# Layer 1 of a four-layer kernel: norm products queued behind an image, x1 stores on two queues, other places in SBUF, a band's weights side by side

## The chip, the cores and the metric

The kernel runs on one core of a Trainium2 chip. A core has five engines, each of which executes its own instructions in order: PE (the matrix engine), DVE and ACT (vector and scalar arithmetic), POOL (general) and SP (which here only issues DMA transfers; POOL and ACT can issue them too). Times are device microseconds (us) of one launch. Lower is better.

## The reference

An input x of shape (4, 8, 512, 512), read as T=4 time steps, B=8 channels and 512 x 512 pixels, goes through four residual layers. Each normalises x by groups of channels (four groups of two), applies an operator and adds the result to x:

```python
x = x + L0(_gn(x))   # spiking attention: q, k, v, scores + relative bias, projection
x = x + L1(_gn(x))   # 13x13 Gaussian, each of the 8 channels by itself, reflected edges
x = x + L2(_gn(x))   # quantised 3x3 convolution, 8 to 8 channels
x = x + L3(_gn(x))   # 3x3 convolution, 8 to 8 channels
```

```python
def _gn(v, G=4, eps=1e-5):
    B_, C_, H_, W_ = v.shape
    g = v.reshape(B_, G, C_ // G, H_, W_)
    m = jnp.mean(g, axis=(2, 3, 4), keepdims=True)
    s = jnp.var(g, axis=(2, 3, 4), keepdims=True)
    return ((g - m) / jnp.sqrt(s + eps)).reshape(v.shape)
```

## The kernel before

Layer 0 runs over 32 steps (b, t), each one attention on one image. Tables of the relative bias (table_own, L476, issued by SP; table_x) are streamed in during each step. What a step leaves is x1, the input of layer 1, written by `project_out` in four chunks c of 128 rows: PE adds up ps_out, ACT copies the input (L862), DVE adds the spikes (L874) and mirrors the edge columns (L879), and DMAs store the rows (L882) and the mirrored edge rows (L887, L890) in DRAM. A step stores 36 pieces and 12 edge rows. In the last two steps, (7,2) and (7,3), which the code calls `late`, POOL issues all of them. The first three chunks of (7,3) lie in a tile of their own, x1_last.

Layer 1 is the class `Layer1`: 32 images n = 4b + t in order. An image lies in one of three buffers xs[n % 3]; `load_image` fills it by four DMAs, and for the first three images a fifth (L1248) fills the spare rows. xs[0] is a part of a tile called raw, which also holds eye (the identity, added to the bands) and the first image's weights bt.

The convolution is made of products with bands: for each image, DVE first forms bt = band · r + eye (L1258; r is 1/deviation of the image's group), then differences d of neighbouring columns in four pieces, two for each half image j (tiles d of a pool d1 of four). PE forms in each half the groups x,bt (odd), d,bt (odd) and d,bt (even), each of 8 matmuls (L1356); the even part of a half is issued after the first group of the next half, from a list `due`. Image 0 is done "plainly" (L1369), without d. ACT moves the results to xo; DVE takes the largest and the smallest value of each half; eight DMAs (L1436) store xo as x2, issued by SP for b = 0 and by POOL for all later b.

```python
if plain:
    self.fetch(1)
    self.offset(0)
self.fetch(n + 2)
```

So image n + 2 is asked for with image n, and `prepare(n + 1)` makes the next bt and d between the halves of image n.

`next_norm(g - 1)` computes the norm of x2's group g - 1 in steps: DVE's sums (L1476 to L1482, L194, L196), a product gps_x on PE (L199) that adds over partitions, DVE again, a second gps_x, and a power on POOL. `group` advances it by t steps after image t of the first channel of group g.

The order of the work is set in three ways. Instructions go to their engine's queue in the order that a list scheduler finds from the program and its priorities. `in_turn` chains those of layer 1 on each engine, by `tc.issue_after(op)`, which places an instruction behind op on op's engine; `self.tails` holds the last of each engine. The framework adds the waits between engines, from the tiles that instructions read and write; a tile that lies over an older tile's place in SBUF waits for the older one's readers and stores.

Where the places overlap before: image 1's buffer x1_0 is at bytes 65696 to 82464 of each partition, d1 (four pieces) at 82464 to 115744, image 2's buffer x1_1 at 115744 to 132512, bt1 at 132512 to 138016. In layer 0, the bias tables lie at 65696 to 97952, x1_last at 112288 to 118576, and the input rows of the last step at 124576 to 132768.

The bands come from `bands1`, run in step n = 1 of layer 0: one DMA (L1214) copies the band rows from SBUF to 16 slanted places in the DRAM array band1d, over a fill with zeros. `start_layer1` loads band1d (L1009) at the end of layer 0. In band1d a row holds, for each of 16 output rows, first the channel, then the pixel offset, then the six bands; the six bands of one pixel are neighbours, so that one band's 64 weights of a matmul lie six elements apart.

Of the kernel before, what the change touches and what calls it, by code (L numbers as in the profile page):

```python
# [35 lines left out]
F32 = mybir.dt.float32  # L36
# [5 lines left out]
ALU = mybir.AluOpType  # L42
# [3 lines left out]
P = 128  # L46
# [11 lines left out]
K1, R1 = 13, 6  # L58
# [234 lines left out]
def layer0(  # L293
# [532 lines left out]
    def project_out(so, c, xt, b, t):  # L826


        dst = x1d[t][b]
        ps = ps_mm.tile([P, D], F32, tag="mm", name="ps_out")  # L830
        late = b == B - 1 and t >= T - 2
        pool_, tag, n_bufs = (x_raw, "sums", 3) if late else (work, "so", 1)
        tokens = pool_.tile([P, NC, P], F32R, tag=tag, name="so", bufs=n_bufs)
        with tc.issue_after(placed[-1]) if placed and not late else ExitStack():
            nc.scalar.copy(tokens, so[:, :, t % 2, ::-1][:, :, c * P : (c + 1) * P])
        nc.scalar.copy(ps, c_p)  # L836
        for k in range(NC):
            for z in range(2):
                nc.tensor.matmul(  # L839
                    ps, lhsT=tokens[:, k, :], rhs=wpT[z][:, k, :],  # L840
                    start=False, stop=k == NC - 1 and z == 1, skip_group_check=True,
                )
        h = h_of["p"][:, c, :]
        if x1_last and c < 3:
            x1 = x1_last[0][:, c]
        else:
            x1 = x1p.tile([P, PH, X1_U], F32, tag="x1", name=f"x1s_{b}_{t}_{c}")
        flat = x1.rearrange("p f u -> p (f u)")
        odd = bass.AP(
            flat.tensor, flat.offset + X1_E + 1,  # L850
            [flat.ap[0], [2 * X1_U - 1, 2], [X1_U, 2], [1, NV // 2]],
        )
        halves = [
            (
                xt.rearrange("p (k g) -> p g k", g=2 * PH)[:, 2 : 2 + PH],
                x1[:, :, 1 : 1 + NV // 2],
            ),
            (xt.rearrange("p (k q f) -> p q f k", q=PH, f=2)[:, ::-3], odd),
        ]
        for x, own in halves:  # L860
            with tc.issue_after(seeds[-1]):
                op = nc.scalar.copy(own, x)  # L862
        placed.append(op.ins)
        v = work.tile([P, D], F32, tag="v", name="v_p", bufs=2)
        if t == 0:
            nc.vector.tensor_copy(v, ps)
        else:
            nc.vector.scalar_tensor_tensor(v, h, 0.5, ps, op0=ALU.mult, op1=ALU.add)
        for z, (_, own) in enumerate(halves):
            cut = v[:, z * HN : (z + 1) * HN]  # L870
            cut = cut.rearrange("p (f k) -> p f k", f=PH)
            parts = [(cut, own)] if z == 0 else [(cut[:, 2 * e : 2 * e + 2], own[:, e]) for e in range(2)]
            for on, to in parts:
                nc.vector.scalar_tensor_tensor(to, on, 1.0, to, op0=ALU.is_ge, op1=ALU.add)  # L874
            nc.vector.bn_stats(st1[b // PAIR][:, t, b % PAIR, c, z, :], own)
        if t < T - 1:
            nc.vector.scalar_tensor_tensor(h, v, 1.0, v, op0=ALU.is_lt, op1=ALU.mult)
        for to, of in MIRRORED:
            (nc.vector if late else nc.gpsimd).tensor_copy(pair(flat, *to), pair(flat, *of))  # L879
        cuts = [0, *range(W1_OUT - R1, P, W1_OUT), P]  # L880
        for first, end in zip(cuts, cuts[1:]):
            op = nc.gpsimd.dma_start(x1_rows(dst, R1 + c * P + first, end - first), x1[first:end])  # L882
        stored.append(op.ins)
        edge = nc.gpsimd if late else nc.sync
        for n in range(R1):
            if c == 0:
                edge.dma_start(x1_rows(dst, n, 1), x1[R1 - n : R1 - n + 1])  # L887
            if c == NC - 1:
                row = P - 1 - R1 + n
                edge.dma_start(x1_rows(dst, X1_R - 1 - n, 1), x1[row : row + 1])  # L890
# [101 lines left out]

    def start_layer1():

        band = shared.tile([P, W1_OUT, B, PH, BANDS], F32, tag="sums", name="band1")
        n_x, n_b = W1_N * X1_U, W1_OUT * BANDS * PH
        raw = shared.tile([P, n_x + 2 * n_b], F32, tag="raw", name="x1_0_0")
        x = raw[:, :n_x].rearrange("p (w u) -> p w u", u=X1_U)
        eye, bt = (
            raw[:, n_x + k * n_b : n_x + (k + 1) * n_b].rearrange("p (m z) -> p m z", z=BANDS)  # L1000
            for k in range(2)
        )
        load_image(nc, x, x1d[0][0], True)
        nc.sync.dma_start(
            eye.rearrange("p m z -> p (m z)"), i["c128"][:, i["c128"].shape[1] - n_b :]
        )
        own = band.rearrange("p r c o z -> p (r c o z)")
        for k in range(2):
            nc.sync.dma_start(by_row(own, k, M1, own.ap[1:]), band1d[k * M1 : (k + 1) * M1])  # L1009
        scale = small0.tile([P, 2], F32, name="scale_1")  # L1010
        nc.vector.tensor_copy(scale[:, 0:1], r1[:, 0, 0:1])
        nc.vector.tensor_scalar_mul(scale[:, 1:2], scale[:, 0:1], -1.0)
        for z in range(SHIFTS):
            out, same = (x[:, :, z].rearrange("p (r o) -> p r o", o=PH) for x in (bt, eye))
            nc.vector.scalar_tensor_tensor(
                out, band[:, :, 0, :, z], scale[:, z % 2 : z % 2 + 1], same,
                op0=ALU.mult, op1=ALU.subtract if z % 2 else ALU.add,
            )
        return band, eye, x, bt
# [153 lines left out]
def bands1(tc, i, band1d, w_sum, psum, state):  # L1173
# [37 lines left out]
    for z in (0, 2):  # L1211
        nc.vector.tensor_sub(to[:, :, SHIFTS + z // 2], to[:, :, z], to[:, :, z + 1])
    row = W1_OUT * n_m
    nc.sync.dma_start(  # L1214
        bass.AP(band1d.tensor, band1d.offset, [[row, n_p], [PH * row + n_m, W1_OUT], [1, n_m]]),
        band.unsqueeze(1).to_broadcast([n_p, W1_OUT, n_m]),
    )

    nc.vector.tensor_reduce(rows, w1, AX.X, ALU.add)
    nc.vector.memset(zeros[:K1, :], 1.0)  # L1220
# [8 lines left out]
    return bass.AP(own.tensor, own.offset + first * step, [[2 * step, n], *dims])  # L1229


def load_image(nc, xt, src, fill=False):

    size, n_half, n = X1_W * X1_U, W1_N // 2, N_PS1 * X1_U
    flat = xt.rearrange("p w u -> p (w u)")
    for j in range(N_1):
        for k, n_rows in ((0, M1), (1, K1_P - M1)):
            at = flat[:, j * n :]
            nc.sync.dma_start(
                by_row(at, k, n_rows, [[n_half * X1_U, 2], [1, n]]),  # L1240
                bass.AP(
                    src.tensor, src.offset + (k + j * N_PS1) * X1_U,
                    [[size, n_rows], [n_half * X1_U, 2], [1, n]],
                ),
            )
    if fill:
        n_rows, n = P - K1_P, W1_N * X1_U
        nc.sync.dma_start(  # L1248
            by_row(flat, 2 * (K1_P - M1) + 1, n_rows, [[1, n]]),
            bass.AP(src.tensor, src.offset, [[size, n_rows], [1, n]]),  # L1250
        )


def image_bands(nc, bt, band, b, r, eye):

    out, same = (x.rearrange("p (r o) z -> p r (o z)", o=PH) for x in (bt, eye))
    own = band[:, :, b].rearrange("p r o z -> p r (o z)")
    return nc.vector.scalar_tensor_tensor(out, own, r, same, op0=ALU.mult, op1=ALU.add)  # L1258


class Layer1:
    def __init__(
# [6 lines left out]
        )  # L1269
        self.band, self.eye, x, self.bt, self.stored = head  # L1270
        self.ps_c = s.enter_context(pool("ps_c", 6, space=PSUM))
        self.xs = [x]
        for k in range(2):
            if k == 1:
                self.dp = s.enter_context(pool("d1", 4))
            held = s.enter_context(pool(f"x1_{k}"))
            self.xs.append(held.tile([P, W1_N, X1_U], F32, name=f"x1_{k}"))
        self.bp = s.enter_context(pool("bt1", 2))
        self.op = s.enter_context(pool("o1", 2))
        self.ends, self.sums, self.offs, self.ready = {}, {}, {}, {}  # L1280
        self.last_ends, self.due, self.tails = [], [], {}
# [7 lines left out]
    def fetch(self, n):  # L1289
        if n < B * T:  # L1290
            b, t = divmod(n, T)
            load_image(self.nc, self.xs[n % 3], self.x1d[t][b], n < 3)

    def prepare(self, n):

# [6 lines left out]
        if t == 0:  # L1302
            self.offset(b)
        xt = self.xs[n % 3]
        bt = self.bp.tile([P, M1, BANDS], F32, tag="bt", name=f"bt_{b}_{t}", bufs=3)
        parts = [
            self.dp.tile([P, 2, N_PS1, 2, X1_E - 1], F32, tag="d", name=f"d_{b}_{t}_{j}")
            for j in range(N_1)
        ]
        self.ready[n] = bt, parts  # L1310
# [24 lines left out]
    def image(self, g, b, t):  # L1335
# [16 lines left out]
        def products(ps, bands, src, start):  # L1352

            for z in range(2):
                for q in range(2):
                    mm = nc.tensor.matmul(  # L1356
                        ps[q * M1 : (q + 1) * M1, :], lhsT=bt[:, :, bands[z]],
                        rhs=src(q)[:, :, z : z + n_v],
                        start=start and z == 0, stop=z == 1, skip_group_check=True,
                    )  # L1360
# [2 lines left out]
        def plainly(ps, par, j):  # L1363

            for z in range(SHIFTS):
                at = (par + z) % 2 * X1_E + (par + z) // 2
                for q in range(2):
                    w0 = q * n_half + j * N_PS1
                    mm = nc.tensor.matmul(  # L1369
                        ps[q * M1 : (q + 1) * M1, :], lhsT=bt[:, :, z],  # L1370
                        rhs=xt[:, w0 : w0 + N_PS1, at : at + n_v],
                        start=z == 0, stop=z == SHIFTS - 1, skip_group_check=True,
                    )
# [70 lines left out]
    def group(self, g):  # L1444
# [9 lines left out]
        for b in range(g * PAIR, (g + 1) * PAIR):  # L1454
            for t in range(T):
# [3 lines left out]
                if g > 0 and b % PAIR == 0 and t > 0:  # L1459
                    if t == 1:  # L1460
                        settling = self.next_norm(g - 1)
                    for _ in range(t):
                        next(settling, None)

    def next_norm(self, g):

# [528 lines left out]
```

## Time and profile before

| | before |
|---|---|
| median of 3 runs | 2686.7 us (2684.2 to 2688.89) |
| the profiled execution | 2696.63 us, span 2694.8 us |
| mean granted PE clock | 0.972 |
| PE busy | 2511.3 us (93%) |
| DVE / ACT / POOL busy | 2000.2 / 1379.3 / 1300.5 us |
| layer 0 | 0 to about 1858 us |
| layer 1 | about 1858 to 2310 us |
| layers 2 and 3 | about 2310 to 2695 us |

The profile is one execution, read as times from the start of its span. A line of a group of instructions names the line in the kernel, the engine, the operation, the tile written and the tiles read, how many, and their time; brackets hold the idle time of the engine just before and what ended it. In a line of waits "A <- B" means that A stood idle until B was done. The columns of a line by window are the stretch, its length, busy time and count of PE, PE's weight loads, DVE, ACT and POOL, the granted PE clock, the DMA engines' busy share, and GB/s.

### The profile page before, as it was taken

The page shows a single profiled execution, that of the slowest core. Times are in us where ns is not written, and L with a number is a line of the kernel's source. Part 1 is how long each engine was busy: PE and PEld are TensorE (multiplying, and loading weights), DVE is VectorE, ACT ScalarE, POOL GpSimd, SP SyncE. Part 2 cuts the span into 40 slices and gives each one's busy share as a digit, 9 for nine tenths or more (in the row PEclk, how much of TensorE's full clock was granted, in tenths as well). Part 3 has the DMA queues.
Part 4 walks back from the last instruction along what each step waited for, and adds up shares of the span by engine and source line. Part 5 has one row for each costly group of instructions (what it writes and reads, how often), then busy time and mean ns, then how long its engine had stood idle before and what let it go on. Part 6 is the DMA issues. An engine that isn't in the chain of part 4 may idle for free.

```text
span 2694.8 us, 50814 instructions
## 1 busy us (share of the span) xinstructions
PE 2511.3 (93%) x17628; PEld 1524.4 (57%) x17628; DVE 2000.2 (74%) x4045; ACT 1379.3 (51%) x2417; POOL 1300.5 (48%) x2880
## 2 busy tenths in 40 slices
PE   7899999999999999999999999998689789699999
PEld 4466666665666656666566565665234344344447
DVE  7777889778787787987878777775677687765550
ACT  1454555555545545455544554544245446666653
POOL 3336447446465454744646445465324334554440
PEclk9899999999999999999999999999789899889999
DMA  6553544444534444354452443436678678567755
GB/s 142 150 154 95 133 126 106 135 120 108 141 92 136 119 118 129 91 148 121 114 119 61 121 116 82 119 80 173 173 218 257 204 237 242 149 183 214 211 161 154
DMA packets 329749, 387.62 MB, mean 144 GB/s; under 512 B 43923, under 2 KB 223635, under 8 KB 329315
## 3 DMA queue, kind: packets, MB, share of 16 engines
q1 hardware_dynamic: 276547, 314.50, 42.3%
q0 software_dynamic: 48448, 64.01, 10.3%
q10 hardware_dynamic: 4496, 5.86, 0.8%
q8 instruction: 139, 2.28, 0.4%
q14 instruction: 119, 0.97, 0.1%
HBM read 279.63 MB, written 104.54 MB: 143 GB/s over the span
## 4 chain that ended last, share of the span: by engine, by line
PE 68%; DVE 7%; DMA 6%; ACT 4%; POOL 3%; issue 3%; SPq 0%; ACTq 0%; DVEq 0%; POOLq 0%
PE ps_conv L1873 8%; PE ps_kv_b L608 8%; PE ps_out L839 8%; PE ps_kv_a L608 7%; PE ps_odd L1356 6%; PE ps_q_b L614 5%; PE ps_own L759 4%; PE ps_q_a L614 3%; PE ps_kv_g L608 3%; PE ps_conv L1732 3%; DMA x<-x 3%; PE ps_even L1356 2%; PE ps_x L759 2%; PE ps_kv_e L608 2%; POOL x L882 2%
## 5 line engine op out<-in xcount | busy, mean ns | idle before, releaser
L882 POOL DMA_DIRECT2D x<-x1s x1125 | 599.7, 569 | 89.2 <-issue 56.0
L879 POOL COPY x1s<-x1s 128x2 f32<-128x2 f32 x720 | 128.0, 244 | 376.9 <-DVE x1s L874 264.9
L839 PE MATMUL ps_out<-wp,so 128*128 128x512 f32 x1024 | 298.2, 435 | 5.9 <-ACT ps_out L836 4.1
L608 PE MATMUL ps_kv_a<-w_raw,x_raw 128*128 128x512 f32 x512 | 250.7, 608 | 8.7 <-ACT ps_kv_a L674 7.9
L608 PE MATMUL ps_kv_b<-w_sums,x_sum 128*128 128x512 f32 x512 | 245.1, 600 | 8.5 <-DVE x_sum L980 5.7
L839 PEld LDWEIGHTS ps_out<-wp,so 128*128 128x128 f32 x1024 | 191.4, 189 | 105.1 <-ACT ps_out L836 38.4
L692 POOL TENSOR_TENSOR h_kv<-h_kv,twice 128x512 f32<-128x512 f32 x96 | 130.3, 1391 | 247.1 <-ACT twice L689 247.1
L1436 POOL DMA_DIRECT2D x<-xo x224 | 124.9, 565 | 237.0 <-ACT xo L1287 220.2
L1873 PE MATMUL ps_conv<-x,band_t 32*32 32x512 f32 x6144 | 231.6, 597 | 1.0 <-ACT o L1913 1.0
L759 PE MATMUL ps_own<-table_own,v 128*128 128x256 bf16 x1536 | 193.0, 275 | 19.0 <-DMA table_own<-bias_parts 12.2
L759 PEld LDWEIGHTS <-v 128*128 128x128 fp8e4 x1536 | 148.7, 98 | 60.1 <-DMA table_own<-bias_parts 24.2
L862 ACT COPY x1s<-xr 128x256 f32<-128x256 f32 x250 | 170.1, 682 | 19.0 <-DVE k L658 6.4
L1768 DVE SCALAR_TENSOR_TENSOR x<-ps_conv,inv,x 128x512 f32<-128x512 f32 x128 | 95.2, 750 | 102.9 <-PE ps_conv L1732 94.0
L1287 DVE TENSOR_TENSOR d<-x 128x1040 f32<-128x1040 f32 x124 | 147.9, 1235 | 30.3 <-DMA x<-x_last 24.7
L795 ACT COPY ps_f<-ps_own 64x512 f32<-64x512 f32 x256 | 142.9, 558 | 43.4 <-PE ps_own L759 16.7
L1873 PEld LDWEIGHTS ps_conv<-x,band_t 32*32 32x32 f32 x6144 | 117.9, 103 | 71.5 <-issue 48.5
L608 PEld LDWEIGHTS ps_kv_b<-w_sums,x_sum 128*128 128x128 f32 x512 | 96.8, 191 | 108.7 <-issue 89.2
L608 PEld LDWEIGHTS ps_kv_a<-w_raw,x_raw 128*128 128x128 f32 x512 | 95.4, 193 | 103.2 <-issue 84.4
L874 DVE SCALAR_TENSOR_TENSOR x1s<-v_p,x1s 128x256 f32<-128x256 f32 x375 | 143.5, 410 | 7.8 <-ACT x1s L862 0.6
L1732 PE MATMUL ps_conv<-xq,band 64*64 64x512 bf16 x1536 | 126.2, 400 | 22.3 <-DVE x L1768 14.4
L1356 PE MATMUL ps_odd<-d,bt 128*64 128x512 f32 x496 | 128.2, 633 | 17.6 <-DVE d L1287 16.5
L1356 PE MATMUL ps_odd<-x,bt 128*64 128x512 f32 x496 | 123.9, 617 | 20.0 <-issue 10.4
(288 smaller groups left out, 5468.9 us busy)
## 6 DMA issues: line engine op xcount, KB each, us to landing
table_own<-bias_parts SPq DMA_DIRECT2D x128, 576.0 KB
x<-x SPq DMA_DIRECT2D x64, 524.0 KB
xq<-in_x SPq DMA_DIRECT2D x128, 256.0 KB
xr<-in_x SPq DMA_DIRECT2D x128, 256.0 KB
out<-o SPq DMA_DIRECT2D x120, 256.0 KB
xs<-in_x SPq DMA_DIRECT2D x112, 256.0 KB
x<-xo POOLq DMA_DIRECT2D x224, 128.0 KB, 4.9
x<-x SPq DMA_DIRECT2D x128, 224.0 KB
```

The costliest lines, as they stand in the source:

```text
L608: mm = nc.tensor.matmul(ps, lhsT=x[:, kk, cc * P : (cc + 1) * P], rhs=w[:, :2, kk, :], start=start and kk == 0, stop=kk == 1, skip_group_c ...
L614: mm = nc.tensor.matmul(ps[:, c, :], lhsT=w[:, 2, kk, c * P : (c + 1) * P], rhs=x[:, kk, :], start=start and c == 0 and kk == 0, stop=kk = ...
L759: nc.tensor.matmul(out, lhsT=src[:, c, h].rearrange("p t e -> p (t e)"), rhs=table[:, z, u : u + HN], start=start and c == 0 and z == 0, s ...
L795: nc.scalar.copy(final[j][a][two * DH : (two + 1) * DH, :], rows[a * DH : (a + 1) * DH, :])
L839: nc.tensor.matmul(ps, lhsT=tokens[:, k, :], rhs=wpT[z][:, k, :], start=False, stop=k == NC - 1 and z == 1, skip_group_check=True,)
L862: op = nc.scalar.copy(own, x)
L874: nc.vector.scalar_tensor_tensor(to, on, 1.0, to, op0=ALU.is_ge, op1=ALU.add)
L882: op = nc.gpsimd.dma_start(x1_rows(dst, R1 + c * P + first, end - first), x1[first:end])
L1287: self.tails[engine] = issue(*args, **kwargs).ins
L1356: mm = nc.tensor.matmul(ps[q * M1 : (q + 1) * M1, :], lhsT=bt[:, :, bands[z]], rhs=src(q)[:, :, z : z + n_v], start=start and z == 0, stop ...
L1732: mm = nc.tensor.matmul(ps[half, :], lhsT=w["band2"][halves[b], kind, dx, :], rhs=xq[halves[b], j % 2, dx : dx + PH, :], start=dx == 0 and ...
L1873: mm = nc.tensor.matmul(ps[c * QP : (c + 1) * QP, :], lhsT=band[g * QP : (g + 1) * QP, int(last), dx, :], rhs=src[:, dx : dx + PH, :], sta ...
```

## The change

It has five parts.

1. Each step of `next_norm` within a group is issued behind the last instruction so far of PE's and DVE's chains.
2. The x1 stores of step (7,2), rows and edges, are issued by SP instead of POOL; those of (7,3) stay on POOL.
3. Image 1 is loaded by ACT's DMA queue instead of SP's.
4. The pool d1 of four pieces becomes two pools of two, one for odd images (d1_1), allocated first, and one for even ones (d1_0), and the weights' pool bt1 moves ahead. The places are then: d1_1 65696 to 82336, x1_0 82336 to 99104, bt1 99104 to 104608, d1_0 104608 to 121248, x1_1 121248 to 138016.
5. In band1d, band and bt a channel's numbers lie together, and in bt the 64 weights of one band are neighbours. The write of the bands becomes eight DMAs, one for each channel, of pieces of 96 bytes instead of 768. eye keeps its order.

```diff
+        engine = nc.sync if late and t == T - 2 else nc.gpsimd
         cuts = [0, *range(W1_OUT - R1, P, W1_OUT), P]
         for first, end in zip(cuts, cuts[1:]):
-            op = nc.gpsimd.dma_start(x1_rows(dst, R1 + c * P + first, end - first), x1[first:end])
+            op = engine.dma_start(x1_rows(dst, R1 + c * P + first, end - first), x1[first:end])
         stored.append(op.ins)
-        edge = nc.gpsimd if late else nc.sync
+        edge = engine if late else nc.sync
...
-        band = shared.tile([P, W1_OUT, B, PH, BANDS], F32, tag="sums", name="band1")
+        band = shared.tile([P, B, M1, BANDS], F32, tag="sums", name="band1")
...
-        eye, bt = (
-            raw[:, n_x + k * n_b : n_x + (k + 1) * n_b].rearrange("p (m z) -> p m z", z=BANDS)
-            for k in range(2)
-        )
-        load_image(nc, x, x1d[0][0], True)
+        eye = raw[:, n_x : n_x + n_b].rearrange("p (m z) -> p m z", z=BANDS)
+        bt = raw[:, n_x + n_b :].rearrange("p (z m) -> p z m", z=BANDS)
+        load_image(nc.sync, x, x1d[0][0], True)
...
         for z in range(SHIFTS):
-            out, same = (x[:, :, z].rearrange("p (r o) -> p r o", o=PH) for x in (bt, eye))
             nc.vector.scalar_tensor_tensor(
-                out, band[:, :, 0, :, z], scale[:, z % 2 : z % 2 + 1], same,
+                bt[:, z], band[:, 0, :, z], scale[:, z % 2 : z % 2 + 1], eye[:, :, z],
...
-    nc.sync.dma_start(
-        bass.AP(band1d.tensor, band1d.offset, [[row, n_p], [PH * row + n_m, W1_OUT], [1, n_m]]),
-        band.unsqueeze(1).to_broadcast([n_p, W1_OUT, n_m]),
-    )
+    n_c = BANDS * PH
+    for c in range(B):
+        nc.sync.dma_start(
+            bass.AP(
+                band1d.tensor, band1d.offset + c * W1_OUT * n_c,
+                [[row, n_p], [PH * row + n_c, W1_OUT], [1, n_c]],
+            ),
+            band[:, c * n_c : (c + 1) * n_c].unsqueeze(1).to_broadcast([n_p, W1_OUT, n_c]),
+        )
...
-    out, same = (x.rearrange("p (r o) z -> p r (o z)", o=PH) for x in (bt, eye))
-    own = band[:, :, b].rearrange("p r o z -> p r (o z)")
-    return nc.vector.scalar_tensor_tensor(out, own, r, same, op0=ALU.mult, op1=ALU.add)
+    return nc.vector.scalar_tensor_tensor(
+        bt.rearrange("p z m -> p m z"), band[:, b], r, eye, op0=ALU.mult, op1=ALU.add
+    )
...
-        self.xs = [x]
+        self.dp, self.xs = [None, s.enter_context(pool("d1_1", 2))], [x]
         for k in range(2):
             if k == 1:
-                self.dp = s.enter_context(pool("d1", 4))
+                self.bp = s.enter_context(pool("bt1", 2))
+                self.dp[0] = s.enter_context(pool("d1_0", 2))
             held = s.enter_context(pool(f"x1_{k}"))
             self.xs.append(held.tile([P, W1_N, X1_U], F32, name=f"x1_{k}"))
-        self.bp = s.enter_context(pool("bt1", 2))
...
-            load_image(self.nc, self.xs[n % 3], self.x1d[t][b], n < 3)
+            engine = self.nc.scalar if n == 1 else self.nc.sync
+            load_image(engine, self.xs[n % 3], self.x1d[t][b], n < 3)
...
-        bt = self.bp.tile([P, M1, BANDS], F32, tag="bt", name=f"bt_{b}_{t}", bufs=3)
+        bt = self.bp.tile([P, BANDS, M1], F32, tag="bt", name=f"bt_{b}_{t}", bufs=3)
         parts = [
-            self.dp.tile([P, 2, N_PS1, 2, X1_E - 1], F32, tag="d", name=f"d_{b}_{t}_{j}")
+            self.dp[n % 2].tile([P, 2, N_PS1, 2, X1_E - 1], F32, tag="d", name=f"d_{b}_{t}_{j}")
...
-                        ps[q * M1 : (q + 1) * M1, :], lhsT=bt[:, :, bands[z]],
+                        ps[q * M1 : (q + 1) * M1, :], lhsT=bt[:, bands[z]],
...
                     for _ in range(t):
-                        next(settling, None)
+                        with self.tc.issue_after(self.tails["PE"]), self.tc.issue_after(self.tails["DVE"]):
+                            next(settling, None)
```

More of the change, by code (lines that the diff above doesn't have):

```diff
@@ L1006, in start_layer1 @@
         )
-        own = band.rearrange("p r c o z -> p (r c o z)")
+        own = band.rearrange("p c m z -> p (c m z)")
         for k in range(2):
@@ L1229, in by_row, with load_image @@
     return bass.AP(own.tensor, own.offset + first * step, [[2 * step, n], *dims])
-def load_image(nc, xt, src, fill=False):
+def load_image(engine, xt, src, fill=False):
     size, n_half, n = X1_W * X1_U, W1_N // 2, N_PS1 * X1_U
@@ L1238, in load_image @@
             at = flat[:, j * n :]
-            nc.sync.dma_start(
+            engine.dma_start(
                 by_row(at, k, n_rows, [[n_half * X1_U, 2], [1, n]]),
@@ L1247, in load_image @@
         n_rows, n = P - K1_P, W1_N * X1_U
-        nc.sync.dma_start(
+        engine.dma_start(
             by_row(flat, 2 * (K1_P - M1) + 1, n_rows, [[1, n]]),
@@ L1369, in plainly @@
                     mm = nc.tensor.matmul(
-                        ps[q * M1 : (q + 1) * M1, :], lhsT=bt[:, :, z],
+                        ps[q * M1 : (q + 1) * M1, :], lhsT=bt[:, z],
                         rhs=xt[:, w0 : w0 + N_PS1, at : at + n_v],
```

## The prediction

> **What bounds the kernel now.** I read the page first, then the waits of layer 1's stretch, then the order of time around each large wait, then the stretches by window. Part 1 and the head of part 4 of the page:
>
> ```profile
> PE 2511.3 (93%) x17628; PEld 1524.4 (57%) x17628; DVE 2000.2 (74%) x4045; ACT 1379.3 (51%) x2417; POOL 1300.5 (48%) x2880
> ...
> PE 68%; DVE 7%; DMA 6%; ACT 4%; POOL 3%; issue 3%; SPq 0%; ACTq 0%; DVEq 0%; POOLq 0%
> ```
>
> TensorE (PE) is the bound over the whole span; what can be won is the time in which it stands still. Layer 1 is the worst place: from 1858 to 2310 us it is busy 366.3 of 452 us. Its waits (us in total, times, longest):
>
> ```profile
> DVE bt L1258 <- DMA x<-x: 49.9, 6, 9.9
> PE gps_x L199 <- DVE gsum_x L196: 41.5, 10, 13.1
> ...
> DVE d L1287 <- DMA x<-x_last: 24.7, 1, 24.7
> ...
> PE ps_odd L1356 <- DVE d L1287: 16.5, 1, 16.5
> PE ps_odd L1356 <- issue: 10.4, 4, 3.9
> PE ps_odd L1356 <- DMA b<-in_b: 7.8, 1, 7.8
> ```
>
> The second row is the norms: PE stands before the tiny product gps_x. The order of time on PE, then on DVE, shows the first of three such stops:
>
> ```profile
> 1998.31 1.93 PE L1356 MATMUL ps_even<-d,bt 128*64 128x512 f32 x8
> 2008.59 0.59 PE L199 MATMUL gps_x<-gsum_x,avg 128*128 128x4 f32 x2 [8.36 <-DVE gsum_x L196]
> 2010.50 0.58 PE L199 MATMUL gps_x<-gsum_x,avg 128*128 128x4 f32 x2 [1.32 <-DVE gsum_x L196]
> ```
>
> ```profile
> 2005.33 2.38 DVE L1287 TENSOR_TENSOR d<-x 128x1040 f32<-128x1040 f32 x2
> 2007.63 0.18 DVE L1476 TENSOR_REDUCE stats<-total 128x16 f32<-128x32 f32 x1
> ```
>
> PE executes in order: gps_x stands in front of image 9's products, whose d were ready before 2005, while DVE reaches the norm's sums only at 2007.63. The other two stops: 2102.70 to 2115.76 and 2210.68 to 2216.71 us.
>
> The other rows are the start of layer 1. First PE, then POOL:
>
> ```profile
> 1897.51 3.99 PE L1356 MATMUL ps_odd<-d,bt 128*64 128x512 f32 x8 [16.46 <-DVE d L1287]
> 1909.26 3.69 PE L1356 MATMUL ps_odd<-x,bt 128*64 128x512 f32 x8 [7.76 <-DMA b<-in_b]
> ```
>
> ```profile
> 1872.76 3.18 POOL L890 DMA_DIRECT2D x<-x1s  x6
> ...
> 1887.89 6.74 POOL L882 DMA_DIRECT2D x<-x_last  x13 [0.65 <-DMA x<-x_last]
> ```
>
> POOL issues the x1 stores of the last two steps of layer 0 one after another, (7,2) until 1875.8, (7,3) until 1903.8. Image 1's second d is written over the place of x1_last and so waits for its stores. The 7.76 named b<-in_b is image 2's load (the DMAs that landed just then are both): its place overlaps x1_last and xr, its pieces were issued at 1896.10 to 1898.08 and its fill at 1904.20, landing at 1909.06.
>
> **The change part by part.** Sums are against the profiled execution, 2696.6 us (span 2694.8); the median of the runs is 9.9 lower, and I carry the same difference to it.
>
> *Norms.* issue_after puts gps_x behind an image's products (PE) and the norm's sums behind an image's DVE work. The same 2 products, 3.5 us of DVE work and one POOL power per norm remain. A group of 8 products takes 1.733 us undisturbed; by excess over that, with the slow restart after each stop, the stops cost 11.0+1.7+1.1 = 13.8, 15.7+1.7+0.4 = 17.8 and 8.6+1.7+1.1 = 11.5: together 43.1. The granted clock shows the restart (columns: us, busy us of PE, PEld, DVE, ACT, POOL, clock, DMA share, GB/s):
>
> ```profile
> 1950.00:2000.00 50.00, 48.90 (x226) 21.95 (x222) 36.47 (x35) 30.69 (x64) 17.27 (x31) 1.00 0.80 245
> 2000.00:2010.00 10.00, 0.83 (x4) 0.50 (x2) 9.39 (x23) 2.04 (x4) 0.63 (x2) 0.65 0.77 244
> 2102.00:2117.00 15.00, 1.29 (x6) 0.50 (x2) 8.99 (x20) 2.03 (x4) 2.02 (x4) 0.61 0.67 233
> ```
>
> What comes back: the gps_x products in line, 3 × 1.2 = 3.6. What is late next: every third image's bt (L1258) waits for an image load, since eye lies in the tile of xs[0], and costs PE 1 to 6 us (three of them: 3.5 at 2067.8, 5.8 at 2183.9, 1.7 at 2263.5). The stops hid this wait for images 17 and 26; I take 4.5 and 3, and 1 for the rest. Queued behind the later sums are DVE's next bt and d, each 0.6 and 1.2 us; an image takes PE 10.4 and DVE 9.7 us, so a wait of DVE of up to about an image is lent by the d held ahead. 43.1 − 3.6 − 8.5 = **−31**, between −20 and −38.
>
> *Start of layer 1.* With image 1's d and x in other places (d1_1 and x1_0 lie over attention tables, free at about 1853.3 when L835 last reads), its 16.46 goes. Its load goes to ACT: 5 issues × 0.62 = 3.1 us, in ACT's idle time from 1853.3 to 1857.9; beyond it each 1 us of ACT would hold the spike copies of the last step. (7,2)'s 48 stores move to SP: an SP issue takes 0.60 to 0.63 in this stretch, POOL's 0.57, so they end at 1848.4 + 48 × 0.62 = 1878 instead of 1875.8, and are in SP's order ahead of the loads of images 2 and 3 and image 0's store. POOL has only (7,3) and ends 27 us earlier, at 1878 to 1882. SP then issues load 2 (5 × 0.62, to 1881.4), the store of image 0 (8, to 1886.6), load 3 (4, two of which wait for the first two, as at 1881.82 and 1886.32), landing at about 1899. Image 2's bt waits for load 3 by the eye, so its products begin at 1900 against 1909.26: what is late next is the eye. **−8.5**, between 0 (order on SP as before) and −22 (load 3 ahead of the stores).
>
> On the issuing engine a rule of the skill differs from a row. SP's issue is not the shorter one here (0.62 against 0.57). The Trainium skill, "DMA: Bandwidth & Descriptors", section "Issuing engine by pattern", calls the path of the sync and scalar queues generally faster. If it landed as much as 1 us sooner, the last store would end 1 us earlier: the sum moves by under 1 us, since the queue's order decides, not the landing.
>
> *Weights block after image 3* (1931 to 1944.6): kept, 0 ± 4.
>
> *A band's weights side by side.* A weight load of 64 strided columns takes 191 ns by its row and lies under products that follow each other every 216 ns. A load of 128 adjacent columns (L608) takes 189. The page "TensorE: Matmul & The Clock Gate", section on LDWEIGHTS, counts columns alone, P / 1.2: 53 ns for 64, strided or not. By the row, adjacency may save up to half of 190; by the rule nothing changes; either is hidden under the products. I take **−1** (0 to −4) for restarts. DVE's bt keeps its 384 elements; its strided write may cost 0.6 us more at most (its own duration again), hidden by DVE's idle time: 0.
>
> *Band writes.* One DMA at L1214 (832 pieces of 768 bytes, issued at 139.19, landed 4.9 us later) becomes eight of 832 pieces of 96 bytes. SP is in order, and behind them stand the table loads of the attention step, first at 141.94. PE has no slack there:
>
> ```profile
> 150.25 1.48 PE L759 MATMUL ps_own<-table_own,v 128*128 128x256 bf16 x12 [1.12 <-DMA table_own<-bias_parts]
> 158.63 1.48 PE L759 MATMUL ps_own<-table_own,v 128*128 128x256 bf16 x12 [1.75 <-DMA table_own<-bias_parts]
> ```
>
> No row shows eight such writes. From below: they follow each other at 0.62, the last is issued at 144.1, the first table 2.2 us late: +1 to +4. From above: their slanted strides interleave, and if the program takes them for overlapping, each waits for the landing of the one before. Loads 0 and 3 into xs[0], whose strides are as uneven, show such waits. A 32.8-KB store lands in a median 2.0 us, a 128-KB one in 4.9; for 80 KB in small pieces I take 2.4. The first table is then 7 × 2.4 − 2.4 = 14.4 late, less 1 of slack: **+13**; at 4.9 per link, +31. I take the chain, as the loads' waits are the nearest case.
>
> Here a rule speaks against the change. The row: 512-byte packets take 28 ns, 768-byte ones 48. The DMA page, "Specifications", asks for at least 512 bytes and says that below this a read-modify-write occurs. By size alone 6656 pieces at under 28 ns over 16 engines are at most 11.6 us of ring time (before: 832 × 48 / 16 = 2.5); were each priced at double by the rule, 23. Spread over eight links, the second adds 1.5 us to each: +24 instead of +13.
>
> Sum: −31 − 8.5 + 0 − 1 + 13 = −27.5: 2669 for the profiled execution, **2659** for the median.
>
> **The rivals.** *Band writes not chained* (0.25): +3 instead of +13, 2649; with load 3 early as well, 2636. For it: image stores in strips (L1436) follow each other at 0.62 without waiting. Against it: those strides nest, the band's don't.
>
> *Gains handed back* (0.15): the norm's DVE part now waits for a gps_x that PE reaches an image later, and holds bt and d of the next image. A stop then shrinks to some 5 us instead of vanishing, and the start gains nothing as load 3 comes last: −20 + 0 − 1 + 13 = −8, 2679. For it: DVE works 9.7 of each 10.4 us. Against: 36.5 of 50 us before the first stop.
>
> *Chain long enough to lose* (0.12): at price p per link the band writes cost 7p − 3.4. They eat the other 40.5 us from p = 6.3 us. Image loads of 224 KB take 5 to 7 us to land, so p = 7.5 is thinkable: +49, slower by 8.5, 2695. Against it: 80 KB is a third of that, and the whole 624 KB took 4.9.
>
> *Nothing done* (0.03): the scheduler keeps gps_x in front and the same waits stand: 2687.
>
> **How the numbers follow.** Forecast 0.45 (2650 to 2672 alone). The range takes in the unchained case down to 2634 and the handed-back one up to 2682, leaving out the losing case and half of the doubtful edge. A measurement here tells 0.2% (5.4 us) from no change: faster 0.83 (forecast, unchained, most of handed back), same 0.05, slower 0.12.
>
> **What would show it.** Right: gps_x L199 waits under 1 us each inside images 9 to 26, with clock 1.00 there; no wait of DVE d on x_last; image 2's first product near 1900, ended by a load; SP's L882 stores from 1848 to 1878; at about 140 us eight L1214 issues 2.4 us apart and a stop of PE on table_own of some 14 us. Unchained: issues 0.6 apart, stop under 5. Handed back: waits of ps_odd on d or bt where gps_x stood. The prediction is wrong if the norms' waits remain, or if the stop at 140 to 175 us exceeds 40.

## The result and the profile after

The changed kernel takes 2682.7 us (median of 20 runs, 2674.1 to 2689.7) against 2687.9 (20 runs): a ratio of 0.9981, with a 95% interval of 0.9971 to 0.9991. That is 5.2 us less where 28 were forecast, below the 0.2% taken as the limit. The profiled execution of before, shown above, was 9 us longer than its median. A second profile of before has a span of 2682.1, and stands beside it wherever lengths are compared.

Part 1 of the page after:

```profile
PE 2509.2 (94%) x17628; PEld 1483.0 (55%) x17628; DVE 2007.7 (75%) x4045; ACT 1377.8 (51%) x2417; POOL 1268.4 (47%) x2832
```

The weight loads (PEld) are 41 us shorter, and it bought nothing, since they lie under the products. The waits of layer 1 after:

```profile
DVE bt L1259 <- DMA x<-x: 75.8, 9, 34.9
...
ACT x1s L862 <- DMA x<-x1s: 19.6, 2, 14.7
PE gps_x L199 <- DVE gsum_x L196: 16.3, 7, 3.9
...
PE gps_x L199 <- DMA x<-x: 5.7, 1, 5.7
ACT xo L1290 <- DMA x<-xo: 5.3, 1, 5.3
```

PE's waits at the norms, the last one of the layer included, went from 41.5 to 22 us (16.3 + 5.7), and d's wait for x_last is gone. What has grown is one wait: the weights bt of an image wait for a load, 75.8 us on DVE instead of 49.9. The window of the first stop before, and the one in which the same norm's products wait now:

```profile
2000.00:2010.00 10.00, 9.87 (x46) 4.00 (x48) 10.00 (x11) 5.11 (x13) 4.44 (x8) 1.00 0.82 250
2030.00:2045.00 15.00, 9.26 (x32) 2.99 (x29) 11.29 (x18) 3.79 (x9) 0.19 (x1) 0.77 0.74 241
```

From 2000 to 2010 PE now works 9.9 of 10 us at full clock. The stop has moved two images on, and became smaller: 5.7 us, at 2037. The list above puts it down to a load itself, and rightly: DVE had waited 4.9 us for that load at the bt of image 11, just ahead of the norm's sums. Stage by stage, in us, with the first product of image n counted from that of image 0:

| | before | before, second profile | after |
|---|---|---|---|
| image 0 starts (end of layer 0) | 1858.9 | 1849.5 | 1855.8 |
| image 2 | 50.4 | 50.0 | 60.6 |
| image 8 | 132.4 | 131.7 | 144.4 |
| image 9 | 155.6 | 154.9 | 154.8 |
| end of layer 1's products | 441.2 | 437.1 | 429.0 |
| from there to the end of the span | 394.7 | 395.5 | 397.4 |

So the start lost 12 to 13 us by image 8, and the stretch of the three norms, image 8 to the end, won 21 to 24. The time of image 2 is the first thing to explain. PE, and then DVE, after:

```profile
1877.71 3.68 PE L1360 MATMUL ps_odd<-d,bt 128*64 128x512 f32 x8 [6.27 <-ACT ps_even L1290]
...
1916.40 3.68 PE L1360 MATMUL ps_odd<-x,bt 128*64 128x512 f32 x8 [28.91 <-DVE bt L1259]
```

```profile
1915.42 0.88 DVE L1259 SCALAR_TENSOR_TENSOR bt<-band,r,x 128x384 f32<-128x384 f32 x1 [34.92 <-DMA x<-x]
```

The bt of image 2 reads eye, which lies in the tile of xs[0], into which image 3 is being loaded. SP's order of time shows when that load could be issued:

```profile
1844.67 11.71 SPq L883 DMA_DIRECT2D x<-x1s  x9
1856.43 4.97 SPq L888 DMA_DIRECT2D x<-x1s  x6
1861.71 19.25 SPq L883 DMA_DIRECT2D x<-x1s  x27
1881.01 4.03 SPq L891 DMA_DIRECT2D x<-x1s  x6
1885.42 8.27 SPq L1242 DMA_DIRECT2D x<-x  x4
1893.74 0.59 SPq L1251 DMA_DIRECT2D x<-x  x1
1894.43 9.01 SPq L1440 DMA_DIRECT2D x<-xo  x8
1903.81 9.80 SPq L1242 DMA_DIRECT2D x<-x  x8
```

The order is the one that was forecast: 48 stores, load 2, the store of image 0, load 3 (the last line holds load 4 too). The stores began on time, 11.1 us before image 0 (forecast: 10.5), but took 40.4 us instead of 48 × 0.62 = 30, load 2 took 9 instead of 3, and the store of image 0 took 9 instead of 5. So load 3 was issued 48 us after image 0 began, where 28 was forecast.

The program shows why. The DMAs of SP and ACT take turns on eight completion semaphores, and a DMA waits until the one before it on its semaphore has landed, whichever engine issued that one. While SP issued the stores, ACT issued image 1's load:

```profile
1849.52 6.52 ACTq L1242 DMA_DIRECT2D x<-x  x4
```

SP's own waits within the stores, and then those from 1884 to 1912:

```profile
SPq L883 <- DMA x<-x: 5.6, 1, 5.6
SPq L888 <- DMA x<-x: 0.6, 1, 0.6
```

```profile
SPq L1242 <- DMA parts<-in_c: 5.0, 1, 5.0
SPq L1242 <- DMA x<-x: 3.6, 2, 3.2
SPq L1440 <- DMA x<-x: 3.0, 3, 1.8
SPq L1440 <- DMA wall<-in_w: 0.9, 1, 0.9
```

The stores waited 6.2 us for pieces of image 1's load. parts and wall belong to the weights block for layers 2 and 3, which ACT issues too. None of these has data in common with the DMA that waited. (The 3.0 are pieces of load 2 on the semaphores of image 0's store; the 3.6 are load 3's last two pieces, which wait for its first two, as forecast.) A run below in which SP issues load 1, `eye_load_sp`, needed 32.4 us for the same 48 stores, so that some 8 of the 10 us come from the load on ACT.

ACT in turn waited for SP's stores, which hold the buffer x1s of its copies:

```profile
1864.17 1.35 ACT L862 COPY x1s<-xr 128x256 f32<-128x256 f32 x2 [14.68 <-DMA x<-x1s]
```

This held back image 0's results on ACT, and PE 6.27 us at image 1 (the first PE line above). It did not hold SP, which waited 0.3 us for ACT.

### The profile page after: what moved, and what is told of

Same layout as the page of the kernel before. It is cut to its first block, busy times and chain, and to the rows that moved or that the text cites. A ratio compares the mean times of both kernels' runs of the same rounds, so it can differ in the third digit from the quotient of the medians.

```text
span 2682.2 us, 51040 instructions
## 1 busy us (share of the span) xinstructions
PE 2509.2 (94%) x17628; PEld 1483.0 (55%) x17628; DVE 2007.7 (75%) x4045; ACT 1377.8 (51%) x2417; POOL 1268.4 (47%) x2832
## 5 line engine op out<-in xcount | busy, mean ns | idle before, releaser
L883 POOL DMA_DIRECT2D x<-x1s x1089 | 579.9, 571 | 50.6 <-POOL x1s L879 30.1
L759 PEld LDWEIGHTS <-v 128*128 128x128 fp8e4 x1536 | 149.4, 98 | 57.6 <-issue 17.2
L835 ACT CAST so<-q 128x512 fp32r<-128x512 fp8e4 x128 | 78.9, 618 | 116.7 <-PE ps_out L839 112.5
```

Of the source, the lines that this page charges most:

```text
L759: nc.tensor.matmul(out, lhsT=src[:, c, h].rearrange("p t e -> p (t e)"), rhs=table[:, z, u : u + HN], start=start and c == 0 and z == 0, s ...
L883: op = engine.dma_start(x1_rows(dst, R1 + c * P + first, end - first), x1[first:end])
```

## The experiments

Ratios are to the kernel before, from the runs that shared its chip. Runs on different chips are compared by ratio (0.001 is 2.7 us).

**The parts alone, with the eye in its place.** `norms_alone` is before with only the issue_after lines:

```diff
-                        next(settling, None)
+                        with self.tc.issue_after(self.tails["PE"]), self.tc.issue_after(self.tails["DVE"]):
+                            next(settling, None)
```

> Kernel before with only the norms' products and sums queued behind an image. Theory E: the three stops go, of 43 us some 20 come back as waits for the eye and one for POOL, so about 20 us below before: 2668 us (2660 to 2676). Rival R: what the order saves it gives back in DVE's and POOL's queues: 2682 to 2690.

Measured: 2667.2 against 2684.1, ratio 0.9939 (0.9922 to 0.9955), 17 us less. This part by itself is a gain, more than three times that of the whole change.

`start_alone` is before with the store, place and load parts of the diff:

> Kernel before with only the stores of (7,2) on SP, image 1's load on ACT and the other places; norms and bands as before. Theory E: image 2 starts some 10 us later, since the load of image 3, for which its bt waits, is now behind 48 stores and image 0's store on SP; the first norm's stop is no longer than before: 5 to 12 us above before, 2693 to 2700. Rival R2 (the start gains what was forecast and the loss lies elsewhere): 8 us below, 2680.

Measured: 2694.0, ratio 1.0042 (1.0028 to 1.0057), 10 us more. Image 2 stands at 57.6 us from image 0. Two of its waits at the start:

```profile
DVE bt L1259 <- DMA x<-x: 32.6, 1, 32.6
...
PE ps_odd L1358 <- DMA x<-x: 26.2, 1, 26.2
```

`start_pool` is the same with the stores of (7,2) back on POOL:

```diff
-        engine = nc.sync if late and t == T - 2 else nc.gpsimd
+        engine = nc.gpsimd
```

> Kernel before with the other places and image 1's load on ACT, all late stores on POOL, norms and bands as before. Theory S (on SP the stores delay the loads of images 2 and 3; POOL's x_last stores delay image 2's d): d of image 2 waits for the last x_last store until about 1894, near where before had image 2 at 1909; loads 2 and 3 long landed; within 4 us of before, some 8 us below start_alone. Rival (ACT's load is what delays the start): as slow as start_alone, about 10 us above before.

Measured: ratio 0.9992 (0.9983 to 1.0002), 2 us less than before and some 13 (9 to 18) less than start_alone. So the load on ACT costs nothing while the stores are on POOL; the loss comes with the stores on SP, where the two hold each other up. (No run has both on SP with the eye in its old place.) The expectation had the wrong wait: bt waited here too, for 22.7 us, but image 2 began at 44.1 us instead of 57.6 after image 0, because load 3 was issued from 31.8 us on and not from 45.9. SP's issues of loads 3 and 4 in start_alone, and then in start_pool:

```profile
1899.66 9.50 SPq L1240 DMA_DIRECT2D x<-x  x8
```

```profile
1882.24 10.45 SPq L1240 DMA_DIRECT2D x<-x  x8
```

**The eye taken out.** `after_eye` moves eye and the first bt out of the image's tile into the free end of the band's tile:

```diff
-        raw = shared.tile([P, n_x + 2 * n_b], F32, tag="raw", name="x1_0_0")
-        x = raw[:, :n_x].rearrange("p (w u) -> p w u", u=X1_U)
-        eye = raw[:, n_x : n_x + n_b].rearrange("p (m z) -> p m z", z=BANDS)
-        bt = raw[:, n_x + n_b :].rearrange("p (z m) -> p z m", z=BANDS)
+        x = shared.tile([P, W1_N, X1_U], F32, tag="raw", name="x1_0_0")
+        sums = shared.tile([P, (B + 2) * n_b], F32, tag="sums", name="band1")
+        band = sums[:, : B * n_b].rearrange("p (c m z) -> p c m z", c=B, z=BANDS)
+        eye = sums[:, B * n_b : (B + 1) * n_b].rearrange("p (m z) -> p m z", z=BANDS)
+        bt = sums[:, (B + 1) * n_b :].rearrange("p (z m) -> p z m", z=BANDS)
```

> Theory E (the eye): what took the gains back is that image n's bt, for n = 2, 5, 8, ..., waits for the load of image n+1, because eye lies in the tile of that load's buffer. In the profile after, image 2 stood 28.9 us for it though its own load had landed some 14 us earlier, image 11 lost 5.7 us and 3.5 more to a slow clock, and images 8, 17, 23, 26 another 7.4. With eye and the first bt beside the band, that goes: 25 to 35 us below the kernel after, about 2653 us, ratio to before near 0.987, and no wait of DVE bt on a load of more than 1 us except at image 2. Rival R (the order of the norms and of the stores costs what it saves, the eye only shows it): under 10 us below the kernel after, 2673 us or more, and PE then waits for bt, d or ACT at the same images.

Measured: 2636.9, ratio 0.9826 (0.9809 to 0.9842), 47 us below before and some 42 below the changed kernel: more than theory E asked for. Layer 1's products take 386.4 us. The norms' waits in its list:

```profile
PE gps_x L199 <- DVE gsum_x L196: 1.8, 1, 1.8
```

No row of bt waiting for a load is left, and images 9 to 31 follow each other at 10.4 to 10.9 us.

`before_eye` makes the same move in the kernel before:

> Kernel before with only eye and the first bt moved from the tile of xs[0] to the place beside the band. Theory E2 (the long norm stops of before were the eye's too: bt of image 8, 16-17 and 26 waits for a load, DVE is in order, and so reaches the norm's sums late; in eye_no_norms the gps_x stand in the old places and cost only 2.6 us of standing each): the three stops shrink to 2 to 3 us each and the other waits for loads go, image 2 starts 5 us sooner at most; 30 to 40 us below before, ratio near 0.987. Rival (the stops come from the placing of gps_x alone): under 15 us below before.

Measured: 2657.9, ratio 0.9895 (0.9881 to 0.9910), 27 us less, a little under what was expected: a new stop of 9.6 us came at image 5, where ACT waits for stores of xo. So this one move, which the change does not make, is worth five times the change.

`eye_no_norms` is after_eye without the issue_after lines:

> Kernel after with eye and first bt beside the band, but the norms' steps placed as before. Theory E (the norms' order is worth its 40 us, and only the eye took half of it back): 35 to 43 us above the version with the eye alone (2636.9), about 2675 us. Rival (the order is worth what norms_alone showed, 17 us, whatever the eye does): about 2654 us.

Measured: ratio 0.9855 (0.9838 to 0.9873), 8 us above after_eye, with an interval of about 1 to 14; layer 1's products take 12.6 us longer in the two profiles. Both expectations fall. The gps_x stand in the same places among PE's products as in the kernel before, yet PE hardly stops:

```profile
1998.79 0.39 PE L199 MATMUL gps_x<-gsum_x,avg 128*128 128x4 f32 x2 [1.32 <-DVE gsum_x L196]
2000.49 0.59 PE L199 MATMUL gps_x<-gsum_x,avg 128*128 128x4 f32 x2 [1.32 <-DVE gsum_x L196]
```

The reason is in DVE's order of time in the kernel before, a few us ahead of its first stop:

```profile
1990.60 0.62 DVE L1258 SCALAR_TENSOR_TENSOR bt<-band,r,x 128x384 f32<-128x384 f32 x1 [9.37 <-DMA x<-x]
```

DVE lost 9.4 us at the bt of image 8 and came that much later to the norm's sums. The stop of 8.36 us was the eye's wait, passed on. This led to the theory tried in before_eye, and that run bears it out. Up to the end of layer 1's products it has

```profile
PE gps_x L199 <- DVE gsum_x L196: 12.8, 8, 3.0
```

where before has 36 us (41.5 less the last norm's 5.4). The first waits of the three stops, 8.4, 13.1 and 6.0 us in before, are 1.2 to 1.4 us each, with gps_x in the same places among the products.

**The parts on top of after_eye.** `eye_pool` has all late stores on POOL:

> Kernel after with eye and first bt beside the band, all late x1 stores on POOL as before. Theory S (the move of the 48 stores holds the loads on SP and is worth nothing once the places are changed): load 2 is issued near 1870, but image 2's d still waits for the last stores of x1_last near 1894; image 2 within 3 us of where it was, total 2634 to 2640. Rival (the second queue does shorten the start): 8 to 15 us above 2636.9, near 2648.

Measured: ratio 0.9869 (0.9850 to 0.9889), about 12 us (5 to 18) above after_eye. The rival holds. The line names d, which began at 1906.1, when the last stores of x_last had landed; POOL had issued these at 1898.9 and 1900.0:

```profile
1907.53 3.49 PE L1360 MATMUL ps_odd<-d,bt 128*64 128x512 f32 x7 [22.14 <-DVE d L1290]
```

The same edit, stores on SP, costs about 13 us while bt waits for load 3 and wins about 12 once it doesn't.

`eye_load_sp` has image 1's load on SP (`engine = self.nc.sync`):

> Kernel after with eye and first bt beside the band, image 1's load on SP instead of ACT. Theory A (ACT's queue is held by the load): ACT's copies of the last chunk of (7,2) come some 8 us sooner against the start of layer 1, the last x1 store and load 2 with them, image 2 some 5 us sooner: about 2632. Rival (on SP the load waits for the attention's last read of q and holds the 48 stores behind it): image 1 and 2 later, 2640 to 2645.

Measured: ratio 0.9840 (0.9818 to 0.9861), not to be told from after_eye. Image 1 stood 19.5 us for its load, image 2 followed at once: the stop changed its place.

`eye_old_bands` is after_eye with the bands' layout and single write of before:

> Kernel after with eye and first bt beside the band, bands in the order of before and written by one DMA. Theory B (the eight writes cost 3.7 us in step n=1 of layer 0, the only place where the traces with and without differ, and the weights' order nothing): about 4 us below 2636.9, near 2633. Rival (the 9.7 us of bands_alone are all in the bands): near 2627. Rival (side-by-side weights help the products): above 2640.

Measured: ratio 0.9809 (0.9791 to 0.9828). It overlaps after_eye, in the direction of theory B.

**The bands.** `bands_alone` is before with only part 5 of the change:

> Kernel before with only a channel's bands and a band's weights side by side and the eight band writes. In the profile after, the eight writes follow each other 0.4 to 1.4 us apart and PE's stops on the tables add up to 3.5 us against 2.9, so 0 within 4 us of before: 2684 to 2692. If strided weights had cost time in matmuls, it would be below 2683; if the writes cost what was forecast, near 2700.

Measured: ratio 1.0041 (1.0026 to 1.0056), 10 us more, beyond the 3 to 4 us by which this step was longer in the traces with eight writes. It was run again beside its two halves, `bt_only` (weights side by side in bt, one write) and `eight_writes` (the write divided, the layout as before: a loop over the 8 channels with `[[row, n_p], [PH * row + n_m, W1_OUT], [1, n_c]]`):

> The kernel of bands_alone once more. If its 9.7 us are real: 7 to 12 above before. If a part of them was that chip's or that hour's: 3 to 7 us, the sum of eight_writes and bt_only (2 to 3).

> Kernel before with only the 64 weights of a band side by side in bt; band1d, its one write and band as before. Theory B (the cost of bands_alone is its eight writes on SP in step n=1): within 3 us of before. Rival (the order of weights costs or the strided write of DVE costs): about 8 us above before. Rival (it helps PE): 3 us or more below.

> Kernel before with the one band write of L1214 divided into eight of 96-byte pieces; layouts as before. Theory B (the writes are the cost of the bands): 4 to 7 us above before, with the first table loads of step n=1 some 2 us later and PE's stops there larger. Rival (the layout costs): within 2 us of before.

Measured: 1.0019 (1.0010 to 1.0029) for bands_again, 1.0012 (1.0003 to 1.0021) for bt_only, 1.0010 (1.0001 to 1.0019) for eight_writes: 5.2, 3.2 and 2.7 us more. The halves add up to the whole, which is about 5 us. The intervals of the two measurements of the whole meet at their edge (1.0026 and 1.0029); why the first was the larger was not found. In step n = 1, the stretch from 132 to 165 us, before and then bands_alone:

```profile
132.00:165.00 33.00, 29.78 (x209) 22.26 (x208) 20.29 (x43) 18.14 (x33) 0.00 (x0) 1.00 0.56 163
```

```profile
132.00:165.00 33.00, 29.01 (x203) 21.69 (x202) 18.04 (x40) 17.29 (x32) 0.00 (x0) 0.95 0.65 163
```

The DMA engines are busy 0.09 × 33 = 3.0 us longer. Where bt_only's 3 us lie was not found in one profile; the nearest suspect, DVE's bt, is longer by 0.3 us in each of 31 images.

**Towards a better version.** `best_load2` is eye_old_bands with image 2's load on ACT too (`if n in (1, 2)`), `best_store0` is that with image 0's store on POOL (`if b > 0 or t == 0`):

> eye_old_bands with image 2's load on ACT too. Theory L (image 2 waits because its load stands behind the 48 stores on SP and behind transfers of the weights block, with which SP and ACT share completion semaphores): the 14 us stop before image 2 goes, with some 4 us of it back from ACT's own work: about 10 us below eye_old_bands, ratio to before near 0.977. Rival (the place of image 2's buffer or d sets it): within 3 us.

> best_load2 with image 0's store on POOL, which stands idle from about 1885 us. If the stores and loads that share SP still hold image 3 or the weights block, 2 to 6 us below best_load2; if the weights block (about 15 us of PE) and the late stores of image 4 set the rest, within 3 us of it.

Measured: 0.9823 (0.9806 to 0.9840) and 0.9820 (0.9806 to 0.9833), no gain over eye_old_bands. Load 2 did come early, and the stop went from image 2 to image 1. PE and ACT of best_load2:

```profile
1884.86 3.69 PE L1358 MATMUL ps_odd<-d,bt 128*64 128x512 f32 x8 [18.35 <-ACT ps_even L1288]
```

```profile
1866.36 9.10 ACTq L1240 DMA_DIRECT2D x<-x  x4
1878.30 0.54 ACTq L1249 DMA_DIRECT2D x<-x  x1
1878.95 0.71 ACT L1288 ACTIVATE xo<-ps_odd,off 128x512 f32<-128x512 f32 x1 [12.62 <-DMA x<-x]
```

ACT spent 12.6 us issuing five DMAs, 9.4 of it waiting for stores of SP to land, with image 0's results behind them.

`before_again` is the kernel before, once more:

> The kernel before, for a second profile. If the profiled execution of before (2696.6, some 9 us above the median) was long in layer 0, layer 1 again takes about 441 us and image 0 starts near 1852; if it was long in layer 1, layer 1 takes about 434.

Measured: 2683.9; layer 1 took 437.1 us and image 0 began at 1849.5. Of the 12.8 us between the two profiles, 9.4 lie in layer 0 and 4.1 in layer 1. One profile of a kernel of this length does not carry a difference of 5 us.

## Why the prediction was wrong, step by step

- **Start of layer 1: forecast −8.5, measured +12 to +13 at image 8.** This is the step that failed: 21 us, against 22 by which the sum missed (−27.5 forecast, −5 measured); the misses of the norms and the bands nearly cancel. The mechanism was named rightly (the stores ahead of load 3 on SP, and bt of image 2 waiting for load 3 by the eye), but its size had the wrong sign. What failed is the price of SP's queue: 0.62 us for each issue ("They end at 1878", "5 issues", "8"), with nothing for the landing that an issue waits for when a transfer before it on its semaphore, ACT's included, is still under way. The 48 stores took 40.4 us instead of 30, and the thirteen issues behind them 18 instead of 8; load 3 was put at 1899 and landed at 1915.4, on an image 0 three us earlier. bt waited 34.9 us for it, and image 2 came 60.6 us after image 0 where the forecast has 41. The bounds, 0 to −22, excluded a loss: nothing gave "order on SP as before" as the worst case.
- **Norms: forecast −31 (−20 to −38), measured −21 to −24 in the change, −17 alone.** The order did what was said, and the allowance for the eye behind it (8.5) was too small: images 10 and 11 alone took 9.7 us over their 10.4 each. The cause given for the stops was only half of it. gps_x was in front, but DVE came late because bt had waited; with the eye out, the order is worth about 8 us (1 to 14).
- **A cost that was not named:** the norm's power on POOL stands in front of image stores, since its gps_x now comes an image later. At 2247 POOL waited 13.6 us for it, issued 16 stores at once, and ACT's next xo waited 5.3 us and PE 3.5 for them.
- **Band writes: forecast +13 by a chain, measured +3 to +4 in the traces and +2.7 alone.** The chain does not exist: the eight were issued in 6.2 us, the second at 137.15 before the first landed at 139.02. The case of 0.25, "not chained, +3", was right. The Trainium skill, "DMA: Bandwidth & Descriptors", section "Specifications", states a read-modify-write below 512 bytes but no price; the doubling was the prediction's own estimate. Measured, a packet of 96 bytes took 12 ns and one of 768 bytes 42: 5.1 us for the 6656 spread over 16 DMA engines, some 3 us more than before, where the estimate by size alone was at most 11.6.
- **Weights side by side: forecast −1, measured +3 as bt_only.** That the gain is hidden was right: the loads shrank from 191 to about 137 ns and the products kept their 216 ns spacing.
- **Weights block: forecast 0, as measured** within 1 us (image 3 to 4: 26.0 before, 26.8 after).

Term by term: −22.5 + 12.5 + 3.5 = −6.5, with the median at −5. The rival *gains handed back* (0.15) was the nearest, at −8: right that "the start gains nothing as load 3 comes last", wrong in the handing-back place, which was bt at a load and not DVE's share of the norm. That its sum came so close is luck in part: it had +13 for the bands, which cost about 3.5, and 0 for the start, which cost 12.5.

## What to carry to other kernels

Before an order is changed around a wait, follow the waiting engine's own delay back: a stop named for gsum_x was a load's wait from the image before, and a constant kept in the tile of a reloaded buffer was behind both. When transfers move to another queue, list what is behind them there and what each of those holds back, including buffers that only their landing frees, and completion semaphores shared with another queue, by which an issue can wait for a transfer that it has nothing to do with. The same move was worth −12 or +13 us depending on whether anyone waited for the last load in that queue. Moving eye and the first bt, with the change kept, gives 2636.9 us, 1.7% below before.

## What the runs showed of the hardware

- A weight load of 64 fp32 columns takes 191 ns with the columns six elements apart and 137 to 141 ns with them adjacent. The Trainium skill, "TensorE: Matmul & The Clock Gate", section on LDWEIGHTS, counts columns only and would give 53 ns for both; here stride counts.
- DVE's bt, 384 elements a row, takes 611 ns written in order (kernel before) and 902 ns written with a stride of 64 elements (kernel after).
- A DMA packet of 96 bytes took 12 ns and one of 768 bytes 42 ns, in the band writes from SBUF to DRAM.
- SP's and ACT's DMAs held each other up through this program's eight shared completion semaphores: in the kernel after, 6.2 us of SP's stores and 5.0 us of its load 2 for transfers of ACT's; in best_load2, 9.4 us of ACT for stores of SP's.
